# Attention softmax: scale the weighted values of each key block instead of the exponentials

## The chip, the core and the metric

The kernel runs on one core of a Trainium2 chip. A core has engines with queues of their own that run side by side and wait for each other through semaphores: TensorE (PE in the profile; its weight loads are PEld), VectorE (DVE), ScalarE (ACT), GpSimd (POOL), and SyncE (SP), which issues most of the DMA transfers here. Matmul results land in PSUM, which holds eight banks of 128 x 512 float32; everything else lies in SBUF. The metric is the device time of one execution, in microseconds (us); lower is better.

## The reference

The program is a block of two layers on an input of 8 images, 384 channels, 32 x 32 pixels. All arithmetic is float32. The change touches one part only, the softmax attention of the second layer. What runs around it matters for the time, though, so both are listed.

```python
# layer 0: per image, a state-space scan over the 1024 pixels, forwards and backwards
#   h[t] = exp(delta[t] * A) * h[t-1] + (delta[t] * u[t]) * B[t];  y[t] = sum over 16 states of h[t] * C[t]
# plus a gated 3x3 convolution and a residual
# layer 1: on the tokens t (8 images, T = 1024 tokens, C = 384 channels)
def attention(x, Wqkv, Wproj, bproj):                 # x = layernorm(t)
    q, k, v = split(x @ Wqkv)                         # 6 heads of 64
    scores = einsum('bhqd,bhkd->bhqk', q, k)          # no 1/sqrt(d)
    scores = where(causal, scores, -inf)
    attn = softmax(scores, axis=-1)
    out = einsum('bhqk,bhkd->bhqd', attn, v)
    return concat_heads(out) @ Wproj + bproj
# t = t + attention(layernorm(t));  t = t + feed_forward(layernorm(t))
# (the feed-forward result is zero for images 5 to 7, so the kernel leaves it out there)
```

## The kernel before

The kernel keeps tokens along the free dimension: 384 channels are 3 blocks of 128 partitions (`c`), and each block holds two heads of 64 (`e`). The 1024 tokens are 8 tiles of 128 (`qi` for queries, `j` for keys), four tiles are a half (`g`), and a key block (`kb`) is 512 keys. Since attention is causal, the first half of the queries has one key block, the second has two.

The work of an image is written as a list of short steps. The attention of one image, the preparation of the image after next and the scan of the next image are interleaved, so that the engines have something of each:

```python
for i in range(B):
    rest = [(before_scan, ORDER[i + 2])] if i + 2 < B else []
    rest.append((attention, ORDER[i]))
    lo = (i + 1) * per + 1
    run(slots(lo, lo + per) if i + 1 < B else [], steps_of(*rest))
```

The attention of the last image has no scan beside it. The scan works on units of two states over 512 pixels; there are 96 units per image. Each takes two products on GpSimd, two exponentials on ScalarE, two scans on VectorE and eight transposes on TensorE that add up the states in PSUM:

```python
nc.gpsimd.tensor_tensor(g, ud, bc, ALU.mult)                              # L519, one unit ahead
nc.scalar.activation(da, dl, AF.Exp, scale=amat[...])                     # L532, twice
nc.vector.tensor_tensor_scan(gi, da, gi, first, ALU.mult, ALU.add)        # L537, twice
nc.gpsimd.tensor_copy(carry[...], g[:, :, end])                           # L542, half of the units
nc.gpsimd.tensor_tensor(g, g, bc, ALU.mult)                               # L543
nc.tensor.matmul(out=y[:, j, :], lhsT=g[:, i, chunk(j)], rhs=ident, is_transpose=True, ...)   # L553, eight times
```

PSUM is shared out as follows. A bank asked for without a tag takes the tags `s` and `pt` in turn.

```python
mid = ctx.enter_context(tc.tile_pool(name="mid", bufs=12))     # tiles of 128 x 1024, asked for by mtile()
BANKS = {"y": 1, "da": 2, "s": 2, "pt": 2, "av": 1}
```

The softmax, for a channel block `c` and a half `g` of the queries, is two lists of steps. The first makes the probabilities. Each query tile is finished by itself: maximum and sum per key block, from them a factor per query, head and key block, and then the exponentials are multiplied by it in place.

```python
def probabilities(c, g, steps):
    for i in range(QT):                                    # 4 query tiles
        for kb, (k0, k1) in enumerate(blocks):             # 1 or 2 key blocks
            # one step:
            #   pr (128 x 1024, one per head) from mid; nm, rs: [P, 2, nb] from small
            for e in range(2):
                nc.tensor.matmul(out=ss[e], lhsT=q, rhs=k, ...)                      # L701
            ...                                            # the causal mask is added by a matmul, L710
            for e in range(2):
                nc.vector.tensor_reduce(m, s, AX.X, ALU.max, negate=True)            # L721
                nc.scalar.activation(pr, s, AF.Exp, bias=m, accum_out=rs[...])       # L722
            if kb < nb - 1:
                return
            if nb == 1:
                nc.vector.reciprocal(rs, rs)                                         # L728
            else:
                nc.vector.tensor_reduce(low, nm, AX.X, ALU.min)                      # L731
                nc.vector.tensor_tensor(nm, low.to_broadcast(...), nm, ALU.subtract) # L732
                nc.scalar.activation(nm, nm, AF.Exp)                                 # L733
                nc.vector.tensor_tensor(rs, rs, nm, ALU.mult)                        # L734
                nc.vector.tensor_reduce(low, rs, AX.X, ALU.add)                      # L735
                nc.vector.reciprocal(low, low)                                       # L736
                nc.vector.tensor_tensor(rs, nm, low.to_broadcast(...), ALU.mult)     # L737
            for e in range(2):
                for k, (a, z) in enumerate(blocks_of(n)):
                    nc.scalar.activation(pr, pr, AF.Copy, scale=rs[:, e, k : k + 1]) # L741
```

The second turns them (keys onto the partitions) and multiplies by the values. One bank `av` gathers all key tiles of both heads.

```python
def weighted_values(c, g, steps):
    def turned(j):
        for e in range(2):
            for i in ...:
                nc.tensor.transpose(pt[:, chunk(i)], pr[:, chunk(j)], ident)         # L754
            nc.scalar.copy(ptn[:, cols], pt[:, cols])                                # L758
    def weigh(j):
        for e in range(2):
            nc.tensor.matmul(out=av[rows_of(e), cols], lhsT=v, rhs=ptn,              # L767
                             start=(j == 0), stop=(j == last))
    # steps j = 0 .. last: turned(j), then weigh(j - 1); at the end:
    weigh(last)
    nc.scalar.copy(st["o"][:, c, half(g)], st["av"])                                 # L786
```

The steps of `weighted_values` of one group are interleaved with those of `probabilities` of the next:

```python
for c in range(NC):
    for g in range(NH):
        made = []
        probabilities(c, g, made)
        for f in spread_over(made, waiting):
            emit(f)
        waiting = []
        weighted_values(c, g, waiting)
```

The order of the instructions on each engine is then settled when the program is built, by a scheduler that also gives the buffers out; each engine works through its queue in that order.

Of the kernel before, what the change touches and what calls it, by code (L numbers as in the profile page):

```python
# [8 lines left out]
F32 = mybir.dt.float32  # L9
# [40 lines left out]
def kernel(  # L50
# [28 lines left out]
    def ctile(name, shape, dt=F32):  # L79
        return const.tile(shape, dt, name=name, tag=name)  # L80
# [4 lines left out]
    def mtile(name, n=L):  # L85
        return mid.tile([P, n], F32, name=name, tag="mid")
# [16 lines left out]
    def chunk(c):  # L103
        return slice(c * P, (c + 1) * P)
# [47 lines left out]
    make_identity(nc, ident)  # L152
    identb = ctile("identb", [P, P], BF16)
    nc.vector.tensor_copy(identb, ident)
    cmask = ctile("cmask", [P, P])
    make_causal_mask(nc, cmask, mask_val=MASKED)
    cmaskb = ctile("cmaskb", [P, P], BF16)
    nc.vector.tensor_copy(cmaskb, cmask)
# [440 lines left out]
    def attention(b, emit):  # L599
# [78 lines left out]
        def rows_of(e):  # L678
            return slice(e * HD, (e + 1) * HD)

        def probabilities(c, g, steps):


            for i in range(QT):
                qi = g * QT + i
                n = (qi + 1) * P
                blocks = [(k0, min(k0 + HB, n)) for k0 in range(0, n, HB)]
                nb = len(blocks)
                for kb, (k0, k1) in enumerate(blocks):

                    @steps.append
                    def _(i=i, qi=qi, n=n, kb=kb, k0=k0, k1=k1, nb=nb):
                        if kb == 0:
                            for e in range(2):
                                st["pr", c, g, i, e] = mtile(f"pr_{b}_{c}_{qi}_{e}")
                            st["nm"] = small.tile([P, 2, nb], F32, name=f"nm_{b}_{c}_{qi}", tag=f"nm{nb}")
                            st["rs"] = small.tile([P, 2, nb], F32, name=f"rs_{b}_{c}_{qi}", tag=f"rs{nb}")
                        nm, rs = st["nm"], st["rs"]
                        ss = [bank(f"s_{b}_{c}_{qi}_{kb}_{e}", "s") for e in range(2)]
                        for e in range(2):  # L700
                            nc.tensor.matmul(  # L701
                                out=ss[e][:, : k1 - k0],
                                lhsT=st["q"][rows_of(e), c, chunk(qi)],
                                rhs=st["k"][rows_of(e), c, k0:k1],
                                start=True,
                                stop=(k1 < n),
                            )
                        if k1 == n:
                            for e in range(2):
                                nc.tensor.matmul(  # L710
                                    out=ss[e][:, k1 - k0 - P : k1 - k0],
                                    lhsT=identb,
                                    rhs=cmaskb,
                                    start=False,
                                    stop=True,
                                )
                        for e in range(2):
                            s = ss[e][:, : k1 - k0]
                            pr = st["pr", c, g, i, e][:, k0:k1]
                            m = nm[:, e, kb : kb + 1]  # L720
                            nc.vector.tensor_reduce(m, s, AX.X, ALU.max, negate=True)  # L721
                            nc.scalar.activation(  # L722
                                pr, s, AF.Exp, bias=m, accum_out=rs[:, e, kb : kb + 1]
                            )
                        if kb < nb - 1:
                            return
                        if nb == 1:
                            nc.vector.reciprocal(rs, rs)  # L728
                        else:
                            low = small.tile([P, 2, 1], F32, name=f"low_{b}_{c}_{qi}", tag="low")  # L730
                            nc.vector.tensor_reduce(low, nm, AX.X, ALU.min)  # L731
                            nc.vector.tensor_tensor(nm, low.to_broadcast([P, 2, nb]), nm, ALU.subtract)  # L732
                            nc.scalar.activation(nm, nm, AF.Exp)  # L733
                            nc.vector.tensor_tensor(rs, rs, nm, ALU.mult)  # L734
                            nc.vector.tensor_reduce(low, rs, AX.X, ALU.add)  # L735
                            nc.vector.reciprocal(low, low)  # L736
                            nc.vector.tensor_tensor(rs, nm, low.to_broadcast([P, 2, nb]), ALU.mult)  # L737
                        for e in range(2):
                            for k, (a, z) in enumerate(blocks_of(n)):
                                pr = st["pr", c, g, i, e][:, a:z]  # L740
                                nc.scalar.activation(pr, pr, AF.Copy, scale=rs[:, e, k : k + 1])  # L741

        def blocks_of(n):
            return [(k0, min(k0 + HB, n)) for k0 in range(0, n, HB)]

        def weighted_values(c, g, steps):
            last = (g + 1) * QT - 1

            def turned(j):
                cols = slice(max(j - g * QT, 0) * P, HB)  # L750
                for e in range(2):
                    pt = bank(f"pt_{b}_{c}_{g}_{j}_{e}", "pt")
                    for i in range(max(j - g * QT, 0), QT):
                        nc.tensor.transpose(  # L754
                            pt[:, chunk(i)], st["pr", c, g, i, e][:, chunk(j)], ident
                        )
                    ptn = ptp.tile([P, HB], F32, name=f"ptn_{b}_{c}_{g}_{j}_{e}", tag=f"ptn{e}")
                    nc.scalar.copy(ptn[:, cols], pt[:, cols])  # L758
                    st["ptn", j, e] = ptn

            def weigh(j):
                if j == 0:
                    st["av"] = bank(f"av_{b}_{c}_{g}", "av")
                cols = slice(max(j - g * QT, 0) * P, HB)
                for e in range(2):
                    hd = 2 * c + e
                    nc.tensor.matmul(  # L767
                        out=st["av"][rows_of(e), cols],
                        lhsT=st["v"][:, j, hd * HD : (hd + 1) * HD],
                        rhs=st["ptn", j, e][:, cols],  # L770
                        start=(j == 0),
                        stop=(j == last),
                    )

            for j in range(last + 1):

                @steps.append
                def _(j=j):
                    turned(j)
                    if j > 0:  # L780
                        weigh(j - 1)

            @steps.append
            def _():
                weigh(last)
                nc.scalar.copy(st["o"][:, c, half(g)], st["av"])  # L786

        waiting = []
        for c in range(NC):
# [261 lines left out]
```

## Time and profile before

The median of three runs is 5526.28 us (5518.49 to 5527.46). The profiled execution spans 5531.4 us. The largest groups of instructions, by the page:

| group | engine | count | busy us | mean ns |
|---|---|---|---|---|
| scan, first product (L519) | GpSimd | 768 | 1847.9 | 2406 |
| scan, second product (L543) | GpSimd | 768 | 1815.5 | 2364 |
| scan, exponentials (L532) | ScalarE | 1536 | 1051.0 | 691 |
| scan itself (L537), two forms | VectorE | 1536 | 1864.5 | 1271 and 1211 |
| scan, transposes (L553) | TensorE | 6144 | 1073.3 | 326 |
| softmax, scores (L701) | TensorE | 1152 | 516.4 | 656 |
| softmax, values (L767) | TensorE | 1152 | 426.5 | 550 |
| softmax, transposes (L754) | TensorE | 1728 | 352.0 | 312 |
| softmax, exponentials (L722) | ScalarE | 576 | 329.5 | 575 |
| softmax, scaling (L741) | ScalarE | 576 | 312.9 | 606 |
| softmax, maxima (L721) | VectorE | 576 | 307.6 | 548 |

A float32 matmul that is not a transpose leaves two records, which is why the 576 score matmuls are counted 1152 times.

How to read it: a line of a group names the kernel's line, the engine, the operation, what it writes and reads, the shapes and the count; then its busy time and the mean of one; then how long the engine sat idle just before its instructions, and what ended that idle time. Windows give the busy time of each engine in a stretch of time. Idle time of an engine counts only if something that sets the end hangs on it, so a saving is looked for in the stage where it falls, and on the chain of waits there.

### The profile page before, as it was taken

To read this page: it belongs to the slowest core of one execution; us is meant where nothing else is said; L and a number is where in the kernel's file an instruction comes from. 1 tells how busy PE (TensorE), PEld (TensorE's weight loads), DVE (VectorE), ACT (ScalarE), POOL (GpSimd) and SP (SyncE) were. 2 spreads that over 40 slices of the span, in tenths; PEclk is the share of its full clock that TensorE was granted. 3 is DMA by queue.
4 is the path that set the end of the run, shared out by engine and by line. 5 is a ranking of instruction groups with operands and counts; after the bars stand their busy time and mean duration, and the time that the engine had idled before them with its cause. 6 is when DMAs were issued, how large, how long until landed. Compare 5 with 4: busy or idle time off the path is not lost. (4 is left out here: it accounts for less than half of the span.)

```text
span 5531.4 us, 49955 instructions
## 1 busy us (share of the span) xinstructions
PE 4355.5 (79%) x15306; PEld 2254.6 (41%) x15306; DVE 3768.4 (68%) x4575; ACT 2941.9 (53%) x5445; POOL 3697.3 (67%) x1932
## 2 busy tenths in 40 slices
PE   5355568887888878888778888788886788788999
PEld 2233334443444434444334444344443444444443
DVE  8777797668766578666686666966669666666422
ACT  6244464666466444664446644556445464565345
POOL 1799878776777637777367774676846977978400
PEclk7576578878888987889878899788997888888988
DMA  5777877657755657557565474664757656656400
GB/s 189 258 262 235 273 251 256 204 185 262 243 184 182 214 182 236 191 173 240 171 234 199 164 243 159 235 205 165 247 168 242 220 191 227 232 190 228 148 15 23
DMA packets 560724, 1124.16 MB, mean 203 GB/s; under 512 B 38424, under 2 KB 78792, under 8 KB 560456
## 3 DMA queue, kind: packets, MB, share of 16 engines
q1 hardware_dynamic: 556896, 1118.97, 60.0%
q8 instruction: 121, 1.98, 0.1%
q10 hardware_dynamic: 3560, 2.00, 0.1%
q14 instruction: 147, 1.20, 0.1%
HBM read 992.90 MB, written 127.93 MB: 203 GB/s over the span
## 5 line engine op out<-in xcount | busy, mean ns | idle before, releaser
L519 POOL TENSOR_TENSOR g<-ud,bc 128x1024 f32<-128x1024 f32 x768 | 1847.9, 2406 | 534.3 <-PE y L553 297.8
L543 POOL TENSOR_TENSOR g<-g,bc 128x1024 f32<-128x1024 f32 x768 | 1815.5, 2364 | 535.0 <-issue 367.9
L532 ACT ACTIVATE da<-dl,amat 128x512 f32<-128x512 f32 x1536 | 1051.0, 691 | 1278.1 <-DVE g L537 1178.4
L553 PE MATMUL y<-ident,g 128*128 128x128 f32 x6144 | 1073.3, 326 | 653.1 <-POOL g L543 637.3
L553 PEld LDWEIGHTS y<-ident,g 128*128 128x128 f32 x6144 | 869.6, 169 | 1037.0 <-POOL g L543 848.6
L537 DVE TENSOR_TENSOR_SCAN g<-da,carry,g 128x512 f32<-128x512 f32 x768 | 955.2, 1271 | 355.8 <-POOL g L519 246.9
L537 DVE TENSOR_TENSOR_SCAN g<-da,g 128x512 f32<-128x512 f32 x768 | 909.3, 1211 | 361.8 <-POOL g L519 259.2
L701 PE MATMUL s<-k,q 64*128 64x512 f32 (+3 forms) x1152 | 516.4, 656 | 137.8 <-ACT pr L722 106.8
L721 DVE TENSOR_REDUCE nm<-s 128x1 f32<-128x512 f32 (+3 forms) x576 | 307.6, 548 | 384.4 <-PE s L710 293.5
L722 ACT ACTIVATE pr<-s,nm 128x512 f32<-128x512 f32 (+3 forms) x576 | 329.5, 575 | 204.6 <-DVE nm L721 201.5
L767 PE MATMUL av<-ptn,v 128*64 128x512 f32 (+3 forms) x1152 | 426.5, 550 | 0.0
L754 PE MATMUL pt<-ident,pr 128*128 128x128 f32 x1728 | 352.0, 312 | 37.8 <-ACT pr L741 32.8
L327 PE MATMUL in<-xn,win 128*128 128x512 f32 x576 | 314.3, 695 | 85.3 <-ACT up L335 42.9
L758 ACT COPY ptn<-pt 128x512 f32<-128x512 f32 (+3 forms) x576 | 261.0, 478 | 205.8 <-PE pt L754 203.0
L542 POOL COPY carry<-g 128x2 f32<-128x2 f32 x384 | 91.1, 237 | 410.4 <-DVE g L537 320.9
L741 ACT ACTIVATE pr<-pr,rs 128x512 f32<-128x512 f32 (+3 forms) x576 | 312.9, 606 | 97.8 <-DVE rs L737 60.0
L918 PE MATMUL yp<-h,w 128*128 128x512 f32 x720 | 320.3, 608 | 39.2 <-DVE h L900 39.2
L754 PEld LDWEIGHTS pt<-ident,pr 128*128 128x128 f32 x1728 | 218.9, 155 | 296.8 <-ACT ptn L758 154.2
L873 PE MATMUL hp<-xf,w 128*128 128x512 f32 x720 | 327.7, 605 | 13.2 <-DVE xf L296 7.1
L701 PEld LDWEIGHTS s<-k,q 64*128 64x128 f32 x1152 | 180.4, 226 | 295.5 <-ACT pr L722 170.6
L645 PE MATMUL qp<-xa,wqk 128*128 128x512 f32 x576 | 259.5, 598 | 15.9 <-DVE xa L296 14.0
L375 DVE SCALAR_TENSOR_TENSOR loc<-xn,vec,loc 128x496 f32<-128x496 f32 (+3 forms) x384 | 253.0, 728 | 0.9
(147 smaller groups left out, 4798.6 us busy)
## 6 DMA issues: line engine op xcount, KB each, us to landing
bc<-rows SPq DMA_DIRECT2D x1536, 512.0 KB, 4.7
t<-st SPq DMA_DIRECT2D x63, 512.0 KB, 6.7
sdl<-dl SPq DMA_DIRECT2D x48, 512.0 KB, 2.7
sud<-G SPq DMA_DIRECT2D x48, 512.0 KB, 3.3
dl<-sdl SPq DMA_DIRECT2D x96, 256.0 KB, 5.3
ud<-sud SPq DMA_DIRECT2D x96, 256.0 KB, 5.4
st<-t SPq DMA_DIRECT2D x39, 512.0 KB, 4.3
xn<-in_x SPq DMA_DIRECT2D x8, 1536.0 KB, 7.2
```

What stands on the lines that cost most here:

```text
L327: nc.tensor.matmul(out=mp, lhsT=st["win"][:, k, chunk(m)], rhs=st["xn"][:, k, half(h)], start=(k == 0), stop=(k == NC - 1),)
L519: pin(nc.gpsimd.tensor_tensor(g, ud, sst.pop(("bc", 0, u.name)), ALU.mult))
L532: nc.scalar.activation(da, sst["dl", u.b, u.c, u.part], AF.Exp, scale=amat[:, u.c, n : n + 1])
L537: nc.vector.tensor_tensor_scan(gi[:, ::step], da[:, ::step], gi[:, ::step], first, ALU.mult, ALU.add)
L543: pin(nc.gpsimd.tensor_tensor(g, g, sst.pop(("bc", 1, u.name)), ALU.mult))
L553: nc.tensor.matmul(out=y[:, j, :], lhsT=g[:, i, chunk(j)], rhs=ident, is_transpose=True, start=(opens and i == 0 and j == 0), stop=(closes ...
L701: nc.tensor.matmul(out=ss[e][:, : k1 - k0], lhsT=st["q"][rows_of(e), c, chunk(qi)], rhs=st["k"][rows_of(e), c, k0:k1], start=True, stop=(k ...
L722: nc.scalar.activation(pr, s, AF.Exp, bias=m, accum_out=rs[:, e, kb : kb + 1])
L754: nc.tensor.transpose(pt[:, chunk(i)], st["pr", c, g, i, e][:, chunk(j)], ident)
L767: nc.tensor.matmul(out=st["av"][rows_of(e), cols], lhsT=st["v"][:, j, hd * HD : (hd + 1) * HD], rhs=st["ptn", j, e][:, cols], start=(j == ...
L873: nc.tensor.matmul(out=hp, lhsT=st["w1"][:, c, chunk(m % 2)], rhs=st["xn"][:, c, half(h)], start=(c == 0), stop=(c == NC - 1),)
L918: nc.tensor.matmul(out=yp, lhsT=st["w2", k // 6][:, k % 6, :], rhs=st["h", k // NC][:, k % NC, half(h)], start=(k == 0), stop=(k == NF - 1),)
```

## The change

The exponentials are no longer scaled before they are turned. They go through the transposes and the values matmul as they are, one key block at a time, and the result of each key block is multiplied by its factor per query. After the transposes, queries lie on the free dimension, so the factors must be turned as well and repeated over the 64 partitions of a head. That is done by a matmul: the factor column of one query tile, broadcast to 64 columns, is the stationary operand and the identity is the moving one. The purpose is to take a pass over all exponentials off ScalarE, to free the transposes from waiting for the statistics, and to compute the statistics once for four query tiles instead of for each.

`probabilities` ends with the exponentials; `nm` and `rs` now hold four query tiles:

```diff
+                        for what in ("nm", "rs"):
+                            st[what, c, g] = small.tile([P, QT, 2, nb], F32, ...)
...
-                        if nb == 1:
-                            nc.vector.reciprocal(rs, rs)
-                        else:
-                            ...                        # L731 to L737
-                        for e in range(2):
-                            for k, (a, z) in enumerate(blocks_of(n)):
-                                pr = st["pr", c, g, i, e][:, a:z]
-                                nc.scalar.activation(pr, pr, AF.Copy, scale=rs[:, e, k : k + 1])
```

`weighted_values` gets the statistics, the turning of the factors, and the scaling:

```diff
+            def factors():
+                nm, rs = st["nm", c, g], st["rs", c, g]
+                st["f", c, g] = mtile(f"f_{b}_{c}_{g}").rearrange("p (k l) -> p k l", k=2)
+                if g == 0:
+                    nc.vector.reciprocal(rs, rs)
+                    return
+                low = small.tile([P, QT, 2, 1], F32, name=f"low_{b}_{c}", tag="low")
+                nc.vector.tensor_reduce(low, nm, AX.X, ALU.min)
+                nc.vector.tensor_tensor(nm, low.to_broadcast([P, QT, 2, 2]), nm, ALU.subtract)
+                nc.scalar.activation(nm, nm, AF.Exp)
+                nc.vector.tensor_tensor(rs, rs, nm, ALU.mult)
+                nc.vector.tensor_reduce(low, rs, AX.X, ALU.add)
+                nc.vector.reciprocal(low, low)
+                nc.vector.tensor_tensor(rs, nm, low.to_broadcast([P, QT, 2, 2]), ALU.mult)
+
+            def spread(kb):
+                fp = bank(f"f_{b}_{c}_{g}_{kb}")
+                for i in range(QT):
+                    for e in range(2):
+                        f = st["rs", c, g][:, i, e, kb : kb + 1]
+                        nc.tensor.matmul(out=fp[rows_of(e), chunk(i)], lhsT=f.to_broadcast([P, HD]),
+                                         rhs=ident, start=True, stop=True)
+                nc.scalar.copy(st["f", c, g][:, kb, :], fp)
...
             def weigh(j):
-                if j == 0:
-                    st["av"] = bank(f"av_{b}_{c}_{g}", "av")
+                if j % QT == 0:
+                    st["av"] = bank(f"av_{b}_{c}_{g}_{j}", "av")
...
-                        start=(j == 0),
-                        stop=(j == last),
+                        start=(j % QT == 0),
+                        stop=(j % QT == QT - 1),
...
+                if j % QT < QT - 1:
+                    return
+                kb = j // QT
+                o, f = st["o"][:, c, half(g)], st["f", c, g][:, kb, :]
+                if kb == 0:
+                    nc.vector.tensor_tensor(o, av, f, ALU.mult)
+                else:
+                    nc.vector.tensor_tensor(av, av, f, ALU.mult)
+                    nc.vector.tensor_tensor(o, o, av, ALU.add)
...
                 def _(j=j):
+                    if j == 0:
+                        factors()
+                    if j % QT == 2:
+                        spread(j // QT)
                     turned(j)
...
                 weigh(last)
-                nc.scalar.copy(st["o"][:, c, half(g)], st["av"])
```

At the setup, the causal mask in float32 moves from a buffer of its own to one of the 12 tiles of the pool `mid`, where it is needed only until its bfloat16 copy is made. The factors `f` take a tile of the same pool for each group.

## The prediction

> **What bounds the kernel now.** I read the busy shares of the page first, to see whether one engine is full.
>
> ```profile
> PE 4355.5 (79%) x15306; PEld 2254.6 (41%) x15306; DVE 3768.4 (68%) x4575; ACT 2941.9 (53%) x5445; POOL 3697.3 (67%) x1932
> ```
>
> None is: the mean hides stages, so I cut the stages by the windows view. Asking for the tile of the exponentials (pr) in stretches of 50 us puts the softmax of the first image at about 970 to 1250 us, that of the second at 1505 to 1800, and that of the last at about 5340 to 5515. The first seven run beside the scan of the next image, the last runs alone. The two kinds (us, then busy time of each engine with its number of instructions, then the clock):
>
> ```profile
> 975.00:1250.00 275.00, 223.98 (x909) 116.59 (x907) 178.72 (x247) 172.78 (x393) 212.19 (x112) 0.79 0.59 196
> ```
>
> ```profile
> 5340.00:5520.00 180.00, 170.66 (x537) 66.13 (x538) 46.63 (x144) 107.91 (x280) 0.00 (x0) 0.82 0.03 10
> ```
>
> Beside the scan, TensorE (81%) and GpSimd (77%) lead, and VectorE (65%) and ScalarE (63%) are far from full, yet TensorE is idle for 51 us of 275. The stage is held by waits between in-order queues, not by one full engine. Alone, TensorE is 95% busy. Next, the waits in the first of these windows (total, times, longest):
>
> ```profile
> PE y L553 <- POOL g L543: 33.5, 14, 3.2
> PE s L701 <- ACT pr L722: 13.0, 9, 3.7
> ACT nm L733 <- DVE nm L732: 11.8, 9, 2.5
> ACT pr L741 <- DVE rs L737: 9.6, 8, 2.0
> PE pt L754 <- ACT pr L741: 3.6, 2, 2.2
> ```
>
> The wait that the change aims at, transposes behind the scaling, is the smallest: 3.6 us. TensorE mostly waits for the scan's product on GpSimd, and the scan hangs on ScalarE (exponentials of the decay) and VectorE (the scan itself). So what the change is worth depends on how much the softmax's small work delays those two queues. The groups of instructions in that window show its size:
>
> ```profile
> L741 ACT ACTIVATE pr<-pr,rs 128x512 f32<-128x512 f32 (+3 forms) x70 | 38.4, 612 | 13.6 <-DVE rs L737 9.6 <-DVE rs L728 4.0
> L732 DVE TENSOR_TENSOR nm<-low,nm 128x4 f32<-128x4 f32 x12 | 13.2, 1102 | 4.4 <-ACT pr L722 4.4
> L737 DVE TENSOR_TENSOR rs<-nm,low 128x4 f32<-128x4 f32 x12 | 10.5, 878 | 0.1
> L734 DVE TENSOR_TENSOR rs<-rs,nm 128x4 f32<-128x4 f32 x12 | 9.6, 799 | 0.9 <-ACT nm L733 0.9
> L733 ACT ACTIVATE nm<-nm 128x4 f32<-128x4 f32 x12 | 2.5, 206 | 12.0 <-DVE nm L732 11.8
> ```
>
> Four elements per partition take VectorE about 1 us. In the last softmax, where GpSimd does nothing, the same operation takes a seventh:
>
> ```profile
> L732 DVE TENSOR_TENSOR nm<-low,nm 128x4 f32<-128x4 f32 x11 | 1.7, 158 | 2.8 <-ACT pr L722 2.8
> ```
>
> Last, the chain of waits, which reaches back over the whole last softmax. From 5340 us to the end (191 us) its shares by line, and the piece before the last group of values can begin:
>
> ```profile
> by line: PE av L767 26.6%; PE s L701 21.9%; PE pt L754 13.7%; ACT pr L741 9.6%; ACT pr L722 8.3%; PE ap L814 6.5%; DVE nm L721 4.4%; PE s L710 2.9%; ACT o L786 1.4%; issue 1.1%; ACT ptn L758 0.7%; DVE t L822 0.4%; DVE rs L728 0.2%; ACT nm L
> ...
> 5491.16 2.56 ACT pr L741 x4
> ```
>
> The scaling is on that chain with 0.096 x 191 = 18.4 us, out of 35.2 us that ScalarE spends on it there (groups of 5345 to 5515): about half of it counts.
>
> **What the Trainium skill says.** Three places bear on this.
> - "SBUF — State Buffer", section "Who interferes with whom": a VectorE instruction with two SBUF inputs contends with a GpSimd instruction that reads SBUF, and the second to come blocks for the whole of the other; with at most one SBUF input it doesn't. The trace agrees: the three small operations with two SBUF inputs take 799 to 1102 ns beside GpSimd's products of 2.35 us, and 158 ns without; the reduction of the same tile (L731) takes about 150 ns in both. The products that the change adds read one operand from PSUM and one from SBUF, so they should stay clear of it.
> - "TensorEngine Tiling (Array Packing)", section "Key Properties": different tiles of the array load and multiply in parallel. The trace agrees: a values matmul of 512 columns that stands alone takes 1.0 us until the next starts, so 384 columns would take 0.75; two of 384 columns, issued as a pair on the two column halves, take 0.80 together. The new matmuls come in such pairs.
> - "Perfetto Trace Analysis", section "Identifying the Most-Contended Engine": matmul busy time is a poor measure of how full TensorE is; the weight loads are better. In the first window these are 116.6 of 275 us. So TensorE has more room than its 81% says, and it can take some new work.
>
> **The change part by part.** Counts are for the whole run, durations from the page's groups; per image is an eighth.
>
> ScalarE. Removed: the 576 scalings, 312.9 us. The 96 small exponentials (19.8 us) become 24, which frees 14.9. The 48 copies of the values (27.6 us) go. Added: 72 copies of the spread factors from PSUM (48 for two key blocks in the second half, 24 for one in the first), at 576 ns like the copy that goes: 41.5 us. Sum: -312.9 - 14.9 - 27.6 + 41.5 = -313.9 us, 39 per image.
>
> VectorE. Seven groups of the statistics (L728 and L731 to L737 without L733) sum to 14.5 + 14.3 + 118.4 + 85.7 + 13.8 + 14.9 + 51.6 = 313.2 us. With four query tiles at once a quarter of the instructions stays, 16 elements instead of 4, nearly the same time each: about 78. Added: 48 products into o, 24 products in place and 24 sums, each 128x512 with one operand in PSUM; the gate's product of that kind takes 673 ns, so 96 x 0.673 = 64.6. Sum: -313.2 + 78.3 + 64.6 = -170 us, 21 per image.
>
> TensorE. Added: 9 spreads per image (three per channel block), each of 8 matmuls, 64 weight columns by 128. A pair of this size is seen in the values matmul:
>
> ```profile
> 1070.60 0.44 PE L767 MATMUL av<-ptn,v 128*64 128x128 f32 x4
> ```
>
> Four records are two matmuls; about 0.27 of the 0.44 is filling, since no such matmul takes under 272 ns. Four pairs at about 0.21 each and one filling give some 1.1 us per spread: 10 us per image, 80 in all. Nothing leaves TensorE.
>
> Waits. Removed: the first transposes of a group behind statistics and scaling, and ScalarE's idle time before L733 and L741 (25.6 us in the first window). New: the values' single bank must be read by VectorE between the two key blocks, 3 times per image, behind a scan of 1.2 us perhaps; and the factors need a buffer of the pool of 12. There 8 tiles of this group and 4 of the next just fitted, the factors make 13, so a tile of the next group waits now and then. I count 3 us per image for both.
>
> On the path. Alone: -18.4 (scaling) - 2.6 (copy of o, 1.4%) + 10 (spreads) + 2 (VectorE's product and sum at the end of groups) = -9 us. Beside the scan: half of ScalarE's 39 us counts, as in the last softmax, -20; of the 25.6 us of idle time and of VectorE's blocked time (36 of the small operations, some 0.8 us too long each, 28 us) three quarters vanish, and I let a third of that reach the path: (25.6 + 28) x 0.75 / 3 = -13; TensorE +10; new waits +3. That is -20 us of some 280. Seven times -20 and -9 make -149 us: 5526 - 149 = 5377, which I round to 5375.
>
> **The rivals.** First, TensorE is the real bound of the softmax stage: 81% busy, and its largest wait is for GpSimd, not ScalarE. Then the freed queues change nothing, and 80 us of spreads with some 24 us of new waits lengthen the run: 5526 + 104 - 20 = about 5610. Against it: weight loads fill 42% only, and in the last softmax, where TensorE is busiest, 18 us of the chain are still ScalarE's scaling. Second, the scan's loop sets the pace: about 45 units of the scan lie in the first window, at 2 x 2.35 us each, so GpSimd needs 212 of 275 us whatever happens. If it still stops for VectorE as often, the gain is the last softmax and little more: 5500. For it speaks GpSimd's 77%; against it, that it idles 63 us there, and waits for a VectorE queue that gets shorter. Third, the queues are so coupled that nearly all of TensorE's 51 idle us go: 275 - 51 + 10 = 234, seven times -41 and -9: about 5230. Fourth, the other order of allocation (one more buffer, more turns of the shared banks) makes new stalls: some us per group, up to 5450 from my 5375.
>
> **Range and chances.** The gain in a stage can lie between 0 and 41 us; the middle is 20, seven times. A third of that either way is 50 us, the waits and a changed order of instructions are worth as much again. So 5265 to 5480 for 8 times in 10. The border of 2% is 5416, 41 us above my number: faster by over 2% 0.63, within 2% 0.33, slower 0.04.
>
> **What would show it.** The scalings (L741) are absent; ScalarE's total is near 2630 us, VectorE's near 3600, TensorE's busy time up by 80 or less. The small statistics still take about 1 us beside GpSimd, but 24 times. A spread takes near 1.1 us. A stretch beside the scan is near 255 us long and GpSimd over 80% busy in it, the last softmax near 171 us instead of 180. I am wrong if TensorE waits for the factors or for VectorE's product of the first key block by several us each, if a scores matmul or its exponential waits for a tile of the pool, or if the stretch stays at 275 us with GpSimd no busier.

## The result and the profile after

The changed kernel takes 5336.75 us (median of 4, 5323.38 to 5340.62), the kernel before 5526.87 us beside it. The ratio is 0.9648, 95% interval 0.962 to 0.9676: 3.5% faster, 38 us below the predicted 5375.

The busy shares of the page after:

```profile
PE 4186.8 (79%) x16458; PEld 2233.8 (42%) x16458; DVE 3620.8 (68%) x4166; ACT 2658.5 (50%) x4822; POOL 3698.2 (69%) x1932
```

ScalarE is down by 283 us and VectorE by 148. TensorE has 1152 instructions more, the spreads, and yet its busy time is down by 169 us. That was not foreseen; the end of this section comes back to it.

The windows view, for the first softmax beside the scan (the stretch shown of before was 275 us long):

```profile
970.00:1225.00 255.00, 212.06 (x1147) 123.92 (x1146) 177.69 (x211) 146.20 (x335) 227.48 (x121) 0.92 0.70 233
```

GpSimd is now 89% busy (227.48 of 255), where it was 77%, and the mean of TensorE's clock in the stretch is 0.92, where it was 0.79. From the first score matmul of an image to its last output projection, read from windows of 5 us, the eight stages took 310, 270, 270, 270, 270, 305, 305 and 210 us before and take 270, 255, 245, 255, 245, 280, 295 and 185 after. The differences sum to 180 of the 199.5 us between the two profiled spans, so the gain lies in these stages: 22 us on average for the seven beside the scan (10 to 40), and 25 for the last.

The waits in that window (total, times, longest):

```profile
...
DVE g L537 <- POOL g L519: 55.5, 35, 4.1
...
PE s L701 <- ACT pr L722: 20.5, 18, 4.0
...
POOL g L519 <- PE y L553: 12.4, 4, 4.7
...
PE f L761 <- ACT pr L722: 6.0, 2, 3.0
...
PE f L761 <- DVE rs L753: 4.0, 2, 2.3
...
PE av L789 <- DVE o L801: 1.7, 1, 1.7
```

The largest wait of TensorE before, 33.5 us for GpSimd's second product, is gone from the list of this window. Instead GpSimd waits for TensorE (12.4 us): it cannot start a product because the transposes have not yet given a buffer back. The same turn shows over the whole run, though not as far. First the kernel before:

```profile
...
PE y L553 <- POOL g L543: 637.3, 261, 11.1
DVE g L537 <- POOL g L519: 506.1, 296, 8.1
...
POOL g L519 <- PE y L553: 297.8, 66, 45.4
...
DVE g L537 <- ACT da L532: 205.5, 115, 7.2
```

and the kernel after:

```profile
...
DVE g L537 <- POOL g L519: 882.2, 501, 7.8
...
POOL g L519 <- PE y L553: 540.3, 157, 45.4
PE y L553 <- POOL g L543: 481.0, 180, 11.1
...
DVE g L537 <- ACT da L532: 19.1, 17, 2.3
```

Before, the scan on VectorE waited 206 us for exponentials from ScalarE; now 19. VectorE waits for GpSimd, and GpSimd more than before for TensorE. TensorE in turn still waits for GpSimd's second product (481 us, where it was 637) more than for anything else. ScalarE has dropped out of the loop of the scan as a cause of waits; TensorE counts for more in it, but no single engine sets its pace.

The new and the shortened groups in the same window:

```profile
L761 PE MATMUL f<-ident,rs 128*64 128x128 f32 x144 | 12.9, 307 | 10.0 <-ACT pr L722 6.0 <-DVE rs L753 4.0
...
L748 DVE TENSOR_TENSOR nm<-low,nm 128x16 f32<-128x16 f32 x3 | 6.0, 2000 | 0.0
L768 ACT COPY f<-f 128x512 f32<-128x512 f32 x9 | 5.2, 579 | 1.3 <-PE f L761 1.2
L750 DVE TENSOR_TENSOR rs<-rs,nm 128x16 f32<-128x16 f32 x3 | 4.1, 1371 | 0.7 <-ACT nm L749 0.7
L801 DVE TENSOR_TENSOR o<-av,f 128x512 f32<-128x512 f32 x6 | 4.0, 674 | 0.0
L753 DVE TENSOR_TENSOR rs<-nm,low 128x16 f32<-128x16 f32 x3 | 3.8, 1273 | 0.1
```

The small operations still take 1.3 to 2 us, but there are 9 of them instead of 36. The product on VectorE (L801) takes 0.67 us and is not stretched. Finally the chain of waits from 5140 us to the end:

```profile
by line: PE s L701 26.2%; PE av L789 22.1%; PE pt L775 14.6%; PE ap L848 8.2%; PE vp L663 5.2%; DVE nm L721 4.9%; PE f L761 4.8%; ACT pr L722 4.6%; PE s L710 3.4%; issue 2.0%; ACT ptn L779 0.9%; DVE t L856 0.4%; DVE o L801 0.4%; ACT f L768 
```

The scaling's 9.6% is gone, the spreads stand on the chain with 4.8% of 192 us, 9.2 us. They do not account for the last stage's 25 us: 18.4 + 2.6 - 9.2 leave 12 us. Two more things changed there. The first is in the timeline of TensorE. Before, in the values of the last image:

```profile
5381.47 1.07 PE L767 MATMUL av<-ptn,v 128*64 128x512 f32 x2
...
5382.47 0.66 PE L754 MATMUL pt<-ident,pr 128*128 128x128 f32 x4
...
5383.06 1.07 PE L767 MATMUL av<-ptn,v 128*64 128x512 f32 x2
```

and after:

```profile
5202.83 1.04 PE L775 MATMUL pt<-ident,pr 128*128 128x128 f32 x8
...
5203.81 1.08 PE L789 MATMUL av<-ptn,v 128*64 128x512 f32 x4
```

Before, the heads alternate: the values of one (two records, 1.0 us to the next start), then the transposes of the other. A key tile takes 2 x 1.59 us. After, eight transposes and then both heads' values stand together, and four records take the 1.0 us that two took, because the heads lie on the two column halves of the array: 0.98 + 1.01 = 1.99 us for a key tile. The instruction order is the scheduler's; the program text asks for neither. In the built order of the whole kernel, 135 pairs of values matmuls stood next to each other before, 195 do after.

The second is TensorE's clock. The profile records the share of full speed that TensorE was granted. In these traces it stands at half or at full, in steps of 3.41 us, and its mean over the run rose. Before, and after:

```profile
core 0: 5531.4 us, clock 0.820
...
core 0: 5331.9 us, clock 0.851
```

At half clock a transpose takes 213 ns to the next start, at full clock 109. The two values records of one head, 1.0 us in the lines above at full clock, take 1.9 us at half; in the last softmax of the kernel before:

```profile
5342.36 1.97 PE L767 MATMUL av<-ptn,v 128*64 128x512 f32 x2
```

So TensorE's busy time can be taken apart. At half clock lay 1372 us of it before and 1045 after; half of that, 686 and 522 us, is time lost to the clock. What remains is its work, counted at full clock: 3669 us before, 3664 after. By this estimate 164 of the 169 us are the clock, and the work as a whole did not shrink: the better order saved about what the spreads cost. The stages show the same, now taken from the start of the first score matmul to the end of the last output projection. The seven beside the scan took 1943 us before, of which 1332 work, 290 lost to half clock and 321 idle, and take 1788 after: 1333, 160 and 295. The last took 202.5 us (153.5, 37.1 and 11.9) and takes 177.2 (153.4, 14.2 and 9.6).

The clock goes with TensorE's waits. In the trace of the kernel before, TensorE was busy less than half the time in 142 of the steps at full clock, and 126 of these were followed by a step at half clock; of 647 steps with over 95% busy none was. From half clock, no step with less than 80% busy (309) was followed by full clock, and 137 of 214 with over 95% were. A long wait of TensorE therefore costs more than its own length: what comes after it runs slowly. No run holds the clock fixed, so its share is read from the traces and not shown by an experiment of its own.

### The profile page after: what moved, and what is told of

Same layout as the page of the kernel before. It is cut to its first block, busy times and chain, and to the rows that moved or that the text cites. A ratio compares the mean times of both kernels' runs of the same rounds, so it can differ in the third digit from the quotient of the medians.

```text
span 5331.9 us, 51307 instructions
## 1 busy us (share of the span) xinstructions
PE 4186.8 (79%) x16458; PEld 2233.8 (42%) x16458; DVE 3620.8 (68%) x4166; ACT 2658.5 (50%) x4822; POOL 3698.2 (69%) x1932
## 4 chain that ended last, share of the span: by engine, by line
POOL 32%; issue 23%; DVE 15%; PE 8%; DMA 5%; ACT 1%; SPq 0%; POOLq 0%; DVEq 0%; ACTq 0%
POOL g L519 17%; POOL g L543 14%; DVE g L537 5%; DMA bc<-rows 4%; DVE loc L375 2%; DVE u L354 2%; DVE dp L465 2%; PE s L701 2%; PE yp L952 1%; PE av L789 1%; POOL carry L542 1%; PE pt L775 1%; PE ap L848 1%; PE op L615 1%; DVE G L479 1%
## 5 line engine op out<-in xcount | busy, mean ns | idle before, releaser
L519 POOL TENSOR_TENSOR g<-ud,bc 128x1024 f32<-128x1024 f32 x768 | 1850.2, 2409 | 817.9 <-PE y L553 540.3
L553 PE MATMUL y<-ident,g 128*128 128x128 f32 x6144 | 1009.7, 315 | 507.7 <-POOL g L543 481.0
L553 PEld LDWEIGHTS y<-ident,g 128*128 128x128 f32 x6144 | 825.8, 162 | 920.6 <-POOL g L543 661.7
L701 PE MATMUL s<-k,q 64*128 64x512 f32 (+3 forms) x1152 | 452.1, 605 | 160.5 <-ACT pr L722 137.6
L789 PE MATMUL av<-ptn,v 128*64 128x512 f32 (+3 forms) x1152 | 351.6, 544 | 23.5 <-DVE o L801 23.2
L775 PE MATMUL pt<-ident,pr 128*128 128x128 f32 x1728 | 307.8, 302 | 63.5 <-ACT ptn L779 39.3
L701 PEld LDWEIGHTS s<-k,q 64*128 64x128 f32 x1152 | 158.1, 207 | 319.7 <-ACT pr L722 215.0
L952 PEld LDWEIGHTS yp<-h,w 128*128 128x128 f32 x720 | 139.8, 195 | 216.7 <-issue 174.6
```

The lines of the kernel that those rows point to most:

```text
L519: pin(nc.gpsimd.tensor_tensor(g, ud, sst.pop(("bc", 0, u.name)), ALU.mult))
L701: nc.tensor.matmul(out=ss[e][:, : k1 - k0], lhsT=st["q"][rows_of(e), c, chunk(qi)], rhs=st["k"][rows_of(e), c, k0:k1], start=True, stop=(k ...
L775: nc.tensor.transpose(pt[:, chunk(i)], st["pr", c, g, i, e][:, chunk(j)], ident)
L789: nc.tensor.matmul(out=av[rows_of(e), cols], lhsT=st["v"][:, j, hd * HD : (hd + 1) * HD], rhs=st["ptn", j, e][:, cols], start=(j % QT == 0 ...
L952: nc.tensor.matmul(out=yp, lhsT=st["w2", k // 6][:, k % 6, :], rhs=st["h", k // NC][:, k % NC, half(h)], start=(k == 0), stop=(k == NF - 1),)
```

## The experiments

Theory A, which carried the prediction: the gain comes from the time that scaling and statistics free in the queues of ScalarE and VectorE. Theory B, its rival: it comes from the order on TensorE. Times are medians; ratios are against the kernel before on the same chip in the same session. The other columns are of the profiled execution: the mean clock, and TensorE's work at full clock, its time lost to half clock and its idle time, in us; these three add up to the span.

| run | us | ratio, 95% interval | clock | work | lost | idle |
|---|---|---|---|---|---|---|
| the kernel before | 5526.87 | | 0.820 | 3669 | 686 | 1176 |
| the change | 5336.75 | 0.9648 (0.962 to 0.9676) | 0.851 | 3664 | 522 | 1145 |
| before, heads paired | 5454.04 | 0.9844 (0.9819 to 0.9868) | 0.817 | 3541 | 683 | 1214 |
| change, heads paired | 5345.94 | 0.9643 (0.9623 to 0.9663) | 0.846 | 3627 | 556 | 1162 |
| change, heads apart | 5482.33 | 0.9895 (0.9872 to 0.9919) | 0.847 | 3808 | 587 | 1101 |
| before, heads apart | 5544.3 | 1.0016 (1.0002 to 1.0031) | 0.834 | 3749 | 623 | 1165 |
| before, no scaling | 5347.14 | 0.9649 (0.9635 to 0.9664) | 0.833 | 3579 | 612 | 1152 |
| before, no scaling, heads apart | 5477.1 | 0.9905 (0.9869 to 0.9941) | 0.838 | 3727 | 617 | 1124 |
| before, no scaling, no statistics | 5193.85 | 0.9378 (0.9356 to 0.9401) | 0.847 | 3604 | 527 | 1062 |
| before, heads paired, statistics for four tiles | 5421.55 | 0.9798 (0.9766 to 0.983) | 0.820 | 3565 | 676 | 1178 |
| change, no spreads | 5262.02 | 0.9503 (0.9477 to 0.9528) | 0.841 | 3587 | 569 | 1100 |
| change, factors turned by transposes | 5297.01 | 0.957 (0.9554 to 0.9586) | 0.847 | 3646 | 535 | 1112 |
| change, small results in PSUM | 5305.31 | 0.9585 (0.957 to 0.96) | 0.852 | 3673 | 518 | 1105 |
| change, both of the last two | 5278.85 | 0.9539 (0.9523 to 0.9555) | 0.849 | 3647 | 525 | 1102 |

**The order alone: heads paired in the kernel before.** `pin` holds an instruction behind the one traced before it on its engine; the values of step j - 1 are traced after the transposes of both heads of step j.

```diff
-                    nc.tensor.matmul(
+                    pin(nc.tensor.matmul(
                         out=st["av"][rows_of(e), cols], ...
-                    )
+                    ))
```

> The kernel before, with one change: the values matmuls of both heads are held behind the transposes of both heads, so that they stand next to each other on TensorE (in the built order 271 neighbouring pairs instead of 135). Theory A (freed queues: the gain comes from the time that the scaling and the statistics leave on ScalarE and VectorE): within 20 us of the 5527 us before, since neither queue is relieved. Theory B (order: the gain comes from TensorE running the two heads side by side, because the scheduler orders it better without the scaling): some 140 more pairs at 0.5 to 1.0 us each are 70 to 140 us, so 5390 to 5460.

Measured 0.9844: 1.6% faster with nothing relieved. Theory A alone is out. It is in theory B's range, but 2.0% short of the change. The clock is as in the kernel before and TensorE's work is 128 us less, so this is an effect of the order itself.

**The same hold in the changed kernel.** The edit is the same.

> The changed kernel with the same hold as in the first of these runs (253 neighbouring pairs instead of 195). Theory A: within 15 us of 5337. Theory B: 60 more pairs at 0.5 to 1.0 us, 30 to 60 us less: 5280 to 5310.

Measured 0.9643, no different from the change. TensorE's work is 37 us less, but it loses 34 us more to half clock and idles 17 us more: what the further pairs save is spent in waits and in the clock.

**Heads forced apart in the changed kernel.**

```diff
-                    turned(j)
-                    if j > 0:
-                        weigh(j - 1)
+                    for e in range(2):
+                        turned(j, e)              # its first transpose pinned
+                        if j > 0:
+                            weigh(j - 1, e)       # pinned
```

> The changed kernel, with the transposes and values of the two heads forced apart (one head's transposes, its values, then the other's; 46 neighbouring pairs instead of 195). Theory A: at most 40 us over the 5337 us of the change, so 5337 to 5380. Theory B: the gain goes: 150 fewer pairs at 0.5 to 1.0 us are 75 to 150 us, so 5410 to 5490.

Measured 0.9895: most of the gain goes. TensorE has 144 us more work and loses 65 us more to half clock, while it idles 45 us less. GpSimd waits longer for it over the whole run than in the change (540.3 us):

```profile
POOL g L519 <- PE y L553: 667.7, 151, 45.6
```

**Heads forced apart in the kernel before.** The edit is the same.

> The kernel before, with the transposes and values of the two heads forced apart as in the split run of the changed kernel (44 neighbouring pairs). If the order on TensorE and the relief of the queues add up independently, the relief is worth the same here as with pairs (5454 to 5346, 108 us), and this takes 5482 + 108 = 5590. If the relief is an effect of the order only, this takes about the 5482 us of the split changed kernel, or less by the spreads.

Measured 1.0016. Both forecasts miss: the time is within 0.3% of the kernel before, where the same order costs the changed one 2.5%. That does not mean that the order costs TensorE nothing here: its work is 79 us more, but it loses 63 us less to half clock and idles 11 us less, and the two nearly cancel. In the last stage, with no scan beside it, the order shows more plainly: 203 us in the kernel before, 174 with heads paired, 221 apart; with the change 177, 165 and 220. There the relief of the queues is worth 9 us with pairs and 1 us with the heads apart.

Over the whole run, with the order held bad the change is worth 1.2% (1.0016 to 0.9895), with it held good 2.0% (0.9844 to 0.9643). So the relief is worth something at either order, the order something in the changed kernel, and the two don't simply add up.

**The scaling left out of the kernel before.** The normalization is missing; the statistics are still computed.

```diff
-                        for e in range(2):
-                            for k, (a, z) in enumerate(blocks_of(n)):
-                                pr = st["pr", c, g, i, e][:, a:z]
-                                nc.scalar.activation(pr, pr, AF.Copy, scale=rs[:, e, k : k + 1])
```

> The kernel before without the scaling of the exponentials (the normalization is left out; the statistics are still computed, per query tile). It frees 313 us of ScalarE and nothing of VectorE, and adds no matmuls. Theory A: ScalarE's part alone: 20 us per image beside the scan and 18 in the last, about 160 us, so 5340 to 5390. Theory B: its built order has 208 neighbouring pairs, as many as the changed kernel, so about the same, 5340 to 5400. If VectorE's statistics were what mattered (a variant of A): above 5430.

Measured 0.9649, as much as the whole change. The built order has 208 neighbouring pairs where the kernel before has 135, and nothing but the scaling is out: so leaving it out also changed the order that the scheduler builds, and the run does not part the two. TensorE's work is 90 us less, its loss to half clock 74 us less and its idle time 24 us less.

**The same with the heads apart**, to take the order out of it:

> The kernel before without the scaling (normalization left out) and with the heads forced apart. It tells how much of the 194 us that the scaling is worth comes from the freed ScalarE with the order of TensorE held bad. If the freed queue acts whatever the order: 5544 less 110 to 190, so 5355 to 5435. If the scaling's worth was mostly the better order: 5480 to 5540.

Measured 0.9905, against 1.0016 with the scaling: about 1.1%, some 60 us, are ScalarE's relief with the order held bad. The rest of the 194 us is gone with the better order. In the waits ScalarE's share is gone here too, and GpSimd waits for TensorE:

```profile
POOL g L519 <- PE y L553: 599.0, 134, 45.0
...
DVE g L537 <- ACT da L532: 43.8, 28, 4.5
```

**Scaling and statistics left out.** The normalization is missing.

> The kernel before without scaling and without statistics (the normalization is left out). Against the run without scaling alone (5347 us) VectorE is relieved of 313 us more. If VectorE's small operations matter once ScalarE is relieved: 5280 to 5320. If not: 5335 to 5355.

Measured 0.9378, 2.7% below the run without scaling: leaving out VectorE's 313 us, and ScalarE's small exponentials (19.8 us) with them, is worth about 150 us, more than twice the most that was forecast (67). TensorE's work is not less (193 neighbouring pairs, where the run with the statistics has 208); it idles 90 us less and loses 85 us less to half clock. The scan on VectorE now waits almost only for GpSimd:

```profile
DVE g L537 <- POOL g L519: 848.6, 503, 6.3
...
DVE g L537 <- ACT da L532: 14.3, 13, 3.2
```

**Statistics for four tiles, scaling kept.** The change's `factors()` without the spreads, followed by the scaling of all exponentials of the group; heads paired, to compare with that run.

```diff
+            def scale(rs):                # called at the end of factors()
+                for i in range(QT):
+                    for e in range(2):
+                        for k, (k0, k1) in enumerate(blocks_of((g * QT + i + 1) * P)):
+                            pr = st["pr", c, g, i, e][:, k0:k1]
+                            nc.scalar.activation(pr, pr, AF.Copy, scale=rs[:, i, e, k : k + 1])
```

> The kernel before with neighbouring pairs, and of the change only the statistics for four query tiles at once; the exponentials are still scaled on ScalarE, all of a group's after its statistics. VectorE gets the relief of 235 us, ScalarE none. If VectorE's small operations carry a part of the gain: 5454 less 20 to 60, 5390 to 5435. If ScalarE's scaling carries it all: 5440 to 5470, or more, since 16 to 24 scalings in a row hold up ScalarE's queue for about 5 to 15 us, three times two per image.

Measured 0.9798 against 0.9844; the intervals overlap, so this run alone does not settle what the statistics are worth. The scalings in a row show as feared, in longer waits of GpSimd for TensorE and of the scan for ScalarE (302.0 and 148.5 us in the paired run):

```profile
POOL g L519 <- PE y L553: 523.6, 25, 76.6
...
DVE g L537 <- ACT da L532: 382.1, 95, 11.4
```

**The spreads left out of the change.** A fixed tile stands in for the factors, so the normalization is missing.

```diff
-                st["f", c, g] = mtile(f"f_{b}_{c}_{g}").rearrange("p (k l) -> p k l", k=2)
+                st["f", c, g] = wout.rearrange("p c e -> p (c e)")[:, : 2 * HB].rearrange(...)
...
-                    if j % QT == 2:
-                        spread(j // QT)
```

> The changed kernel without the matmuls and copies that spread the factors; a fixed tile stands in for the factors (the normalization is left out, the products on VectorE and the statistics stay). If TensorE's time counts fully: 80 us for the spreads and 45 us of waits for their factors less, 5210 to 5270. If half counts: 5280 to 5300. If the spreads lie in TensorE's idle time: 5320 to 5345.

Measured 0.9503: 1.4%, about 80 us, for 72 spreads of about 1.02 us, the waits around them and 72 copies on ScalarE. The time lies in the range that was forecast for work that counts fully, near its upper end: of the 125 us of that forecast less than two thirds arrived. The traces say why: TensorE has 77 us less work and idles 45 us less, as forecast, but gives back 47 us because more of its work falls at half clock (mean clock 0.841, where the change has 0.851).

**A cheaper spread.** ScalarE repeats the factor columns over 64 columns, and four transposes turn them, where eight float32 matmuls did.

```diff
-                for i in range(QT):
-                    for e in range(2):
-                        f = st["rs", c, g][:, i, e, kb : kb + 1]
-                        nc.tensor.matmul(out=fp[rows_of(e), chunk(i)], lhsT=f.to_broadcast([P, HD]), rhs=ident, ...)
+                fw = st["f", c, g][:, kb, :]
+                nc.scalar.copy(fw.rearrange("p (i e d) -> p i e d", e=2, d=HD),
+                               st["rs", c, g][:, :, :, kb : kb + 1].to_broadcast([P, QT, 2, HD]))
+                for i in range(QT):
+                    nc.tensor.transpose(fp[:, chunk(i)], fw[:, chunk(i)], ident)
```

> The changed kernel with a cheaper spread: ScalarE first repeats the factor columns of a key block over 64 columns (one copy of 512 elements), then four transposes turn them, instead of eight float32 matmuls. TensorE saves about 1.02 - 0.45 = 0.57 us per spread, 41 us in all; ScalarE gets 72 copies of some 0.67 us, 48 us. If TensorE sets the pace now (the run without spreads took 75 us less for some 75 us of spreads): 5290 to 5315. If ScalarE's queue still counts as it did before: 5330 to 5350.

Measured 0.957, 0.8% or about 43 us below the change, with more work on ScalarE. The two groups of the whole run:

```profile
L764 PE MATMUL f<-ident,f 128*128 128x128 f32 x288 | 52.5, 309 | 36.4 <-ACT f L759 23.8 <-ACT pr L722 12.6
...
L759 ACT COPY f<-rs 128x512 f32<-128x512 f32 x72 | 42.6, 615 | 23.8 <-DVE rs L753 23.7
```

43 us more on ScalarE cost nothing that can be seen, and the spreads' group takes 44 us less than in the change (96.3). The size of the gain is as forecast, but not by the path of the forecast: TensorE's busy time as a whole falls by 5 us only (4186.8 to 4181.5), and it idles 33 us less. That its saved time alone made the gain is not shown.

**The small results in PSUM.** No small operation reads two operands from SBUF any more.

```diff
-                low = small.tile([P, QT, 2, 1], F32, name=f"low_{b}_{c}", tag="low")
+                ps_ = bank(f"st_{b}_{c}_{g}")
+                low = ps_[:, : 2 * QT].rearrange(...)
+                ex = ps_[:, 2 * QT : 6 * QT].rearrange(...)
                 nc.vector.tensor_reduce(low, nm, AX.X, ALU.min)
                 nc.vector.tensor_tensor(nm, low.to_broadcast([P, QT, 2, 2]), nm, ALU.subtract)
-                nc.scalar.activation(nm, nm, AF.Exp)
-                nc.vector.tensor_tensor(rs, rs, nm, ALU.mult)
+                nc.scalar.activation(ex, nm, AF.Exp)
+                nc.vector.tensor_tensor(rs, rs, ex, ALU.mult)
...
-                nc.vector.tensor_tensor(rs, nm, low.to_broadcast([P, QT, 2, 2]), ALU.mult)
+                nc.vector.tensor_tensor(rs, ex, inv.to_broadcast([P, QT, 2, 2]), ALU.mult)
```

> The changed kernel with the statistics' small results in PSUM, so that no small VectorE operation reads two operands from SBUF. If the blocking by GpSimd is what makes them long, they take 0.15 to 0.25 us instead of 0.8 to 1.2, and VectorE is relieved of some 50 us. At the worth seen without statistics (153 us for 313 us) that is 25 us: 5305 to 5325. If VectorE no longer matters in the changed kernel: 5330 to 5345; a bank more in use could cost up to 15 us.

Measured 0.9585, 0.65% below the change. The groups of the whole run:

```profile
L756 DVE TENSOR_TENSOR rs<-st,low 128x16 f32<-128x16 f32 x24 | 3.9, 164 | 0.4
L752 DVE TENSOR_TENSOR rs<-rs,st 128x16 f32<-128x16 f32 x24 | 3.9, 164 | 5.9 <-ACT st L751 5.6
...
L750 DVE TENSOR_TENSOR nm<-st,nm 128x16 f32<-128x16 f32 x24 | 3.8, 157 | 4.3 <-ACT pr L722 3.8
```

164 ns, beside GpSimd, where the change has 0.8 to 1.2 us in the mean of the run (1225, 923 and 796 ns). This is the section "Who interferes with whom" of the Trainium skill's "SBUF — State Buffer" put to use: with one SBUF input the operation doesn't contend with GpSimd, and the trace agrees.

**Both together.**

> Both of the last two. If they add up: 40 us for the spread and 25 for the statistics less, 5270 to 5290. If TensorE sets the pace alone: as with the cheaper spread, 5290 to 5315.

Measured 0.9539: 1.1% below the change, 4.6% below the kernel before. The two add up, as the first forecast had it. That is the fastest version that computes the reference in full.

## Why the prediction was right, and where it was not

The number held, 5375 for 5337, with the border of 2% well cleared. The path did not hold as well, and the agreement of the stage's sum is partly luck. By its steps:

- *ScalarE -314 us.* The groups came as counted (72 copies at 583 ns), the busy total fell by 283. Instructions overlap a little in the trace: two scalings of 384 columns in a row took 1.12 us where two means make 1.21. The difference of 31 us may be such overlap between groups; that was not followed further.
- *VectorE -170 us.* It fell by 148. The small operations came out at 88 us instead of 78, still stretched, and the products at 65.0, as worked out.
- *A spread costs 1.1 us.* 1.02 us on the chain. 80 us were put in, and leaving the spreads out saved about 80; but that run also took out 45 us of waits and lost 47 us to the clock, so the equality is an accident of these two.
- *New waits, 3 us per image.* Too small. Over the run TensorE waits 23.5 us for the values' bank, 45.3 for the factors, and 15.9 in transposes for the copy of the factors: 85 us, 11 per image. The pool's thirteenth tile is no part of it: exponentials wait 0.4 us in all for transposes, 1.2 before.
- *Half of ScalarE's time, and a third of the idle and blocked time, reach the path: -33 us per image.* The stage's sum (-20, measured -22) came out for a partly wrong reason. By the traces TensorE's work in the seven stages stayed the same, its idle time fell by 26 us and its loss to half clock by 130, so most of the gain came by the clock. The lines that the prediction showed had the clock in them (0.79 and 0.82), and its sum has no term for it. Leaving the scaling out is worth 194 us, but only some 60 with the order of TensorE held bad. And VectorE's small operations, of which I let a third count, are worth about 150 us for 313.
- *Last softmax -9.* Measured -25, of which 23 us are less time at half clock. Two terms are missing: the clock, and the saving by TensorE's new order, which paid for the spreads (the work of the stage is the same, 153.5 and 153.4 us). With heads paired in both kernels the change is worth 9 us here, the predicted sum.
- *TensorE's busy time up by 80 or less.* It fell by 169 us. This is the step that failed: the sum gave TensorE new work only ("Nothing leaves TensorE"), and took the time of its work as fixed. The work stayed the same and 164 us less were lost to half clock.
- *Room on TensorE by its weight loads (42% of the window).* Not borne out: pairing the heads alone takes 131 us off TensorE's busy time and gains 1.6%.
- *The rivals.* The first (TensorE is the real bound, so that freed queues change nothing) is out as it was put: the change gains 1.2% even with the order held bad. But TensorE's time did count, 1.6% by pairs in the kernel before and 2.5% by a bad order in the changed one. The second fell: GpSimd went to 89%. The third, nearly all of TensorE's idle time goes, did not come true: 43 of 255 us are still idle in the first window, after 51 of 275.

The sum in one line, from the ratios at 5527 us: scaling and statistics out -344; the quarter of the statistics that stays and the products on VectorE +69; the spreads +80; together -195. The terms are differences of runs that also differ in clock and order, and the first contains the better order. How it splits between order and queues depends on what the other does: 1.2% for the change with a bad order, 2.0% with a good one, and the order alone 1.6% in the kernel before and 2.5% in the changed one. By the traces the kernel before hardly loses from fewer pairs because the clock gives back what the bad order takes (63 of 79 us); why it does so there and not in the changed kernel is open. The forced orders also move transposes and scores, and that was not tried apart.

## What to carry to other kernels

When several in-order queues are coupled in a loop, relieving one of them changes who waits for whom, so look at the waits again after each step. Look at TensorE's clock beside its busy time: shorter waits can make the same matmuls faster, and a change of busy time is not yet a change of work. Work taken off one engine can also reorder another: compare the instruction order, not only the counts, and hold the order still in an experiment before crediting the relief. Tiny VectorE operations beside a busy GpSimd are not tiny when both inputs lie in SBUF; putting one of them in PSUM gained 0.65% here.

## What the runs showed of the hardware

- Values matmuls of two heads on the two column halves, 512 columns, float32, at full clock: 1.01 us for both when they stand together, 1.0 us for each when transposes stand between them.
- TensorE's granted clock stands at half or full in these traces, in steps of 3.41 us. From full clock, 126 of 142 steps with less than 50% busy were followed by half clock, and none of 647 with over 95%. A float32 transpose of 128 x 128 takes 109 ns to the next start at full clock and 213 at half.
- A VectorE operation on 16 elements per partition took 0.8 to 1.2 us in the mean with two inputs in SBUF beside GpSimd's products, and 0.16 us with one of them in PSUM.
- Turning and repeating four query tiles' factors for two heads: 1.02 us of TensorE by eight float32 matmuls with a broadcast stationary operand (16 records). As four transposes it has 288 records instead of 1152 in the run, busy 52.5 us instead of 96.3.
